# One of four bank assignments, one read and the transposes in a two-layer block-product kernel

## The chip, the cores and the metric

The kernel runs on one NeuronCore of a Trainium2 chip. The metric is the device time of one execution in microseconds. The kernel before took 1352.98 us, the median of three runs (1351.76, 1352.98 and 1362.14). The profile is of a further execution, which took 1365.32 us.

Engines are called as in the profile: PE is TensorE (the matrix engine), PEld its loading of weights, DVE is VectorE, ACT is ScalarE, POOL is GpSimd, and SP is SyncE, which here only issues DMAs. An engine works through its own queue in order. It stops at an instruction until the semaphores that this one waits for have been reached, and all that stands behind it waits too.

## The reference

The input x has 32 batches of 64 channels and 1024 positions. A table of 16 matrices of 64 x 64 is indexed by a condition per batch. A feed-forward layer follows, and its result is added to x.

```python
W = weights[condition]                          # (32, 64, 64)
y = einsum('bct,bcd->bdt', x, W)                # (32, 64, 1024)
h = gelu(einsum('bsd,df->bsf', y, inter_w) + inter_b, approximate=True)   # F = 4096
x + einsum('bsf,fd->bsd', h, output_w) + output_b
```

All is in float32. Seen as matrices, layer one multiplies 2048 x 1024 by 1024 x 4096, layer two 2048 x 4096 by 4096 x 1024.

## The kernel before

**Blocks.** Both layers use a scheme of seven block products in place of eight (sums of blocks are formed first, and each product is added to several results), and use it twice, one inside the other. So 49 small products replace 64. The outer seven stand in `OUTER` (line 25: 1, 2, 6, 7, 4, 5, 3) in the order in which they are computed, the inner seven in `INNER` (lines 30 to 38). A line of `INNER` gives a slot (its time inside the block), the product's number, the PSUM tag, whether it starts a new accumulation, and the sub-block of the result. The state tables (`STATE`, `MID_STATE` and those for the end) say which results a product is added to: X, V, D in layer one, X, Y, Z, D in layer two.

**Passes.** Layer one makes eight passes (`it`): two halves of the rows times four groups of columns. Layer two makes seven outer products (`o` from 0 to 6), and each product there sums over the four groups of columns. A pass is 49 units of time, and a unit is one product. In the trace a product is eight PE rows of 128 x 256, because each float32 matmul shows as two; names beginning with f (`fA`, `fB`, `fC`) are products of layer one, with z of layer two, and the letter after it is the PSUM tag. Names with X, V, D, Y or Z after f or m (`fX`, `mZ`) are results in SBUF.

**PSUM.** [...] The pool `pst` holds two under the tag t, for copies of left and right sums. The pool `acc_pool` holds two for each of the tags A, B and C. `INNER` puts one product per block on B (slot 1, read in slot 2), one accumulation on C (slots 2 and 5, read in slots 3 and 6), and the rest on A. A tag's two banks are given out in turn, and a bank is free when the readers of its former tile are through. VectorE takes one operand of a sum from PSUM, so ScalarE first copies the other operand there (`to_psum`, lines 199 to 207, ACT at L206).

**Order.** The order is written out by hand. `at(time, fn, ...)` (line 177) collects steps, `run` (line 180) sorts them by time and calls them. What a step issues goes to the end of its engines' queues. Times set only the order. A tile is allocated when its step is called.

**Layer one, end of a block.** `hidden` (lines 588 to 644) is called for outer products 2, 4, 5 and 3, whose results are complete. For each of the sub-blocks "11" = (0,0), "21" = (0,1), "22" = (1,1) and "12" = (1,0) it applies the gelu (`do_gelu`, ACT at L569). In the passes of the second half of the rows (`it >= NG`, passes 4 to 7) it then forms an inner sum in place: `inner_s1_copy` copies the lower half of the tile into a C bank, and `inner_s1` adds it to the upper half on VectorE. After these come the outer sums (a1 to a6) and the stores of the results to DRAM (`hs_d`).

**Layer two.** `product3` issues a product, `read3` moves or adds its result: the first time it is a ScalarE copy (L941), otherwise a VectorE sum. `inner_h2` forms inner sums of the left operand (`hs`) from ScalarE copies and VectorE sums. When a block of an outer result is complete, `outer_copy` and `outer3` add the outer results. For outer products 2, 4, 5 and 3 the result then goes out: `transpose` (line 1024) makes four PE transposes into a tile `tp` on a B bank, `add_x` adds it to a tile `xb` of x that `load_xb` has fetched, and `store_out` stores it. The pool of `xb` has four tiles, so a load waits until the store of the tile four before it has landed. In the last blocks the tile of x is called `xe`.

**Queues.** All of layer two's loads are issued by SP: the left operands (`load_h`, L811), the weights (`load_w`, L817), `xb` (L1021), and so are the stores (L1042). GpSimd forms sums of whole left operands and weights (`mid_h`, `mid_w`, `inner_w2`) in the order of the tables `POOL2` and `POOL2_END`, lines 1053 to 1063.

Of the kernel before, what the change touches and what calls it, by code (L numbers as in the profile page):

```python
# [24 lines left out]
OUTER = (1, 2, 6, 7, 4, 5, 3)  # L25
# [50 lines left out]
def kernel(  # L76
# [37 lines left out]
    B, C, T = x.shape  # L114
# [62 lines left out]
    def at(time, fn, *args):  # L177
        steps.append((time, len(steps), fn, args))
# [6 lines left out]
    def add(eng, o, a, b, sub=False):  # L185
        eng.tensor_tensor(o, a, b, ALU.subtract if sub else ALU.add)  # L186
# [12 lines left out]
    def to_psum(src, tag=None):  # L199
        uid[0] += 1  # L200
        pool = late["acc"] if tag else pst
        t = pool.tile([P, 2, W], F32, tag=tag or "t", name=f"t{uid[0]}")
        if len(src.shape) == 2:
            t = t.rearrange("p k n -> p (k n)")
        t = t[:, : src.shape[1]]
        nc.scalar.copy(t, src)  # L206
        return t
# [280 lines left out]
    def y_block(a, p, r):  # L488
        q = Y[a, RIGHT[p]]
        return {"11": blk(q, 0, 0), "21": blk(q, 1, 0)}.get(r) if r in ("11", "21") else YI[a, p][r]  # L490

    def w1_block(it, p, l):
        q = W1[it, LEFT[p]]
        return {"11": lblk(q, 0, 0), "12": lblk(q, 0, 1)}.get(l) if l in ("11", "12") else WI[it, p][l]
# [66 lines left out]
    H = {}  # L561

    def gelu(it, fin, sub):
        s = it % NG
        t = state[fin[0], sub]
        H[it, fin, sub] = t
        for u in range(2):
            f = 8 * s + 4 * fin[1][0] + 2 * sub[0] + u
            nc.scalar.activation(  # L569
                t[:, u, :], t[:, u, :], AF.Gelu_apprx_tanh, bias=b1[:, f : f + 1]  # L570
            )

    S1 = {}

    def inner_s1_copy(it, fin, sub):
        S1[it, fin, sub] = to_psum(H[it, fin, sub][:, 1, :], "C")

    def inner_s1(it, fin, sub):

# [8 lines left out]
    def hidden(base, it, fin):  # L588


        v = nc.vector
        subs = {"11": (0, 0), "12": (1, 0), "21": (0, 1), "22": (1, 1)}
        e = {}

        def get(n):
            H[it, fin, n] = e[n] = H[it, fin, subs[n]]

        def new(n):
            H[it, fin, n] = e[n] = cpool.tile(
                [P, 2, W], F32, tag="c", name=f"h{n}_{it}_{fin[1][0]}{fin[1][1]}"  # L600
            )

        def do_gelu(n):
            gelu(it, fin, subs[n])
            get(n)

        def a1():
            e["p"] = to_psum(e["21"])

        def a2():  # L610
            new("s3")
            add(v, e["s3"], e["11"], e["p"], sub=True)

        def a3():
            add(v, e["21"], e["p"], e["22"])
            H[it, fin, "s1"] = e["s1"] = e["21"]
            e["p"] = to_psum(e["11"])

        def a4():
            new("s2")  # L620
            add(v, e["s2"], e["s1"], e["p"], sub=True)

        def a5():
            e["p"] = to_psum(e["12"])
            new("s4")

        def a6():
            add(v, e["s4"], e["p"], e["s2"], sub=True)

        for n, t in (("11", 2.9), ("21", 6.9), ("22", 7.9), ("12", 12.9)):  # L630
            at(base + t, do_gelu, n)
            if it >= NG:
                at(base + t + 0.01, inner_s1_copy, it, fin, subs[n])
                at(base + t + 0.45, inner_s1, it, fin, subs[n])
        at(base + 8.3, a1)
        at(base + 9.3, a2)
        at(base + 9.6, a3)
        at(base + 10.6, a4)
        at(base + 13.4, a5)
        at(base + 14.4, a6)  # L640
        for n, t in (
            ("11", 4.2), ("22", 9.2), ("s3", 10.5), ("s1", 11), ("s2", 12), ("12", 14.2), ("s4", 15.6),
        ):
            at(base + t, store_h, it, fin, n)
# [52 lines left out]
    for j, i in enumerate(order):  # L697
        t = M_AT[i]
# [18 lines left out]
    for j, t in enumerate(later):  # L717
        i = NR - NL + j
# [14 lines left out]
    for it in range(nit):  # L733
# [5 lines left out]
        for n, t in W_AT.items():  # L739
            if it == 0:  # L740
                t = {1: -10, 2: -3.5, "s3": -3, "s1": -2}.get(n, t)
# [4 lines left out]
        for o, p in enumerate(OUTER):  # L746
# [3 lines left out]
                lambda l, r, it=it, p=p, a=a: (w1_block(it, p, l), y_block(a, p, r)),  # L750
            )
            fin = STATE[p][1]
# [6 lines left out]
        if it == 1:  # L759
            for k in range(KQ):  # L760
                e = {}
                t = b0 + 5 + 10.8 * k
# [3 lines left out]
        elif it >= 2:  # L766
            n = -(-len(w2_pieces) // (nit - 2))
            for j in range(n):
                i = (it - 2) * n + j
                if i < len(w2_pieces):  # L770
                    e = {}
                    t = b0 + 9.5 + 14 * j
# [61 lines left out]
    def mid_s3(time, o, t):  # L834

        e = {}

        def one(k):
            if k == 0:
                pool, tag = (wpool, "w") if (o, t) == (6, 1) else (yq, "yq")  # L840
                HT[o, "s3", t] = pool.tile([P, NG, 2, W], F32, tag=tag, name=f"hs3_{o}_{t}")
            e[k] = to_psum(HT[o, "s2", t][:, k])

        def two(k):
            add(nc.vector, HT[o, "s3", t][:, k], HT[o, "22", t][:, k], e[k], sub=True)

        for k in range(NG):
            at(time + 0.8 * k, one, k)
            at(time + 0.8 * k + 0.6, two, k)
# [59 lines left out]
    def mids(o):  # L909
        return MID_END if o == 6 else MID  # L910
# [36 lines left out]
    def add_copy(time, dst, src):  # L947

        e = {}

        def one():
            e["p"] = to_psum(src(), "C")

        def two():
            add(nc.vector, dst(), e["p"], dst())

        at(time, one)
        at(time + 0.6, two)
# [105 lines left out]
    for o in range(7):  # L1064
        b = end1 + 49 * o
        pick = lambda later, first=None: b + (first if o == 0 else later)
        for (n, t), tt in H_LOAD.items():
            at(pick(*tt), load_h, o, n, t)
        for n, tt in W_LOAD2.items():
            at(pick(*tt), load_w, o, n)  # L1070
        for n, k, *tt in POOL2_END if o == 6 else POOL2:
            if n == "w":
                at(pick(*tt), inner_w2, o, mids(o)[k])
            elif n[0] == "t":
                at(pick(*tt), mid_w, o, n)
            else:
                at(pick(*tt), mid_h, o, n, k)
        mid_s3(b + (18.9 if o == 6 else 24), o, 0)
        mid_s3(b + (22.2 if o == 6 else 28), o, 1)
        for i, q in enumerate(mids(o)):  # L1080
            bq = b + 7 * i
            inner_h2(bq - 2.2 if (o, i) != (0, 0) else bq + 0.7, o, q)
            rs = INNER
            if (o, i) in ((6, 5), (6, 6)):

                at(bq + 7.01, read3, o, i, (6, 7, "A", False, (1, 0)))
                rs = INNER[:-1] + ((7, 4, "B", True, (1, 0)),)
            for r in rs:
                at(bq + r[0], product3, o, i, r)
                at(bq + r[0] + 1, read3, o, i, r)  # L1090
            if q == MID_SUM:
                parts = ((0, slice(0, 2), 7.1), (1, slice(0, 2), 12.1))
                if o == 6:
                    parts = (parts[0], (1, slice(1, 2), 7.2), (1, slice(0, 1), 12.1))
                for t, c, f in parts:
                    add_copy(
                        bq + f,
                        lambda o=o, t=t, c=c: MS[o, "Z", t][:, c, :],
                        lambda o=o, t=t, c=c: MS[o, "X", t][:, c, :],
                    )  # L1100
            for j, (src, mb) in enumerate((MID_DONE_END if o == 6 else MID_DONE).get(q, ())):
                for t in range(2):
                    if (o, i) == (6, 6):

                        add_copy(
                            bq + (1.2, 2.3)[t],
                            lambda o=o, t=t: MS[o, "Z", t],
                            lambda mb=mb, t=t: OS["X", mb, t],
                        )
                        at(bq + 4, ends_in, o, mb, t)  # L1110
                    f = bq + (7.1, 8.1 if (o, i) == (6, 5) else 12.2)[t] + j
                    if (o, i) != (6, 6):
                        at(f, outer_copy, o, src, mb, t)
                        at(f + 0.7, outer3, o, src, mb, t)
                    if STATE[OUTER[o]][1] is None:
                        continue
                    at(b + 33 if (o, mb, t) in ENDS else f - 1.8, load_xb, o, mb, t)
                    if (o, i) == (6, 6):
                        continue
                    at(f + 2.2, transpose, o, mb, t)  # L1120
                    at(f + 3.2, add_x, o, mb, t)
                    at(f + 4, store_out, o, mb, t)
# [52 lines left out]
```

## Time and profile before

| what | us |
|---|---|
| median of three runs | 1352.98 |
| profiled execution | 1365.32 |
| its span, first to last instruction | 1363.5 |
| PE busy | 1340.6 |
| VectorE busy | 882.7 |
| GpSimd busy | 959.7 |
| ScalarE busy | 487.2 |
| mean granted PE clock over the span | 0.991 |

Busy time is the union of an engine's instructions in the profiled execution. A PE row's duration contains its way through the array and overlaps the next row, so the distance from start to start is the better measure of a stream of matmuls. The list of waits gives, for an engine and a line, what ended its idle time, how long that was in total, how often, and the longest. The timeline merges neighbouring instructions of one kind; the number in brackets is the engine's idle time before them and what ended it. The view of stretches gives, for each engine, its busy time and number of instructions, and then the granted PE clock, the mean busy share of the 16 DMA engines, and GB/s.

### The profile page before, as it was taken

The numbers are of one execution on the slowest core, as the hardware profiler recorded it, in microseconds if no ns is written. First come the engines' busy times: TensorE is split into PE (matmuls) and PEld (weight loads), VectorE is DVE, ScalarE is ACT, GpSimd is POOL, SyncE is SP. The second block draws the span as 40 slices with busy tenths as digits, with TensorE's granted clock in tenths as the row PEclk, the third lists the DMA queues.
The fourth block names the chain that finished last, engine by engine and source line by source line (L and its number), as shares of the span: only waits on it lengthen the run. The fifth ranks groups of instructions, "written<-read, shape, count | busy, mean of one in ns | idle before, by whom it ended". The sixth has DMA issues, their size and how long they took to land.

```text
span 1363.5 us, 19040 instructions
## 1 busy us (share of the span) xinstructions
PE 1340.6 (98%) x6572; PEld 1174.7 (86%) x6572; DVE 882.7 (65%) x1581; ACT 487.2 (36%) x985; POOL 959.7 (70%) x599
## 2 busy tenths in 40 slices
PE   8899999999999999999999999999999999999998
PEld 8788888888888888888888888888888888888887
DVE  1757457575687765756647674775766757767676
ACT  1533324233254341533515332433334333333341
POOL 3772954948659587495762976958959689496692
PEclk7999999999999999999999999999999999999999
DMA  5655578586898767667659236173270723917611
GB/s 194 197 172 190 172 219 286 208 288 220 284 362 273 237 218 248 241 222 244 229 191 332 70 123 264 45 296 139 96 275 7 290 97 112 359 32 257 222 47 62
DMA packets 135472, 273.40 MB, mean 201 GB/s; under 512 B 15728, under 2 KB 68208, under 8 KB 123728
## 3 DMA queue, kind: packets, MB, share of 16 engines
q1 hardware_dynamic: 134336, 271.53, 57.4%
q8 instruction: 53, 0.87, 0.2%
q0 software_dynamic: 448, 0.46, 0.1%
q14 instruction: 43, 0.35, 0.1%
q10 hardware_dynamic: 592, 0.20, 0.1%
HBM read 167.28 MB, written 104.86 MB: 200 GB/s over the span
## 4 chain that ended last, share of the span: by engine, by line
PE 53%; DVE 2%; POOL 1%; DMA 1%; issue 1%; ACT 1%; SPq 0%; DVEq 0%; ACTq 0%; POOLq 0%
PE zA L555 24%; PE zC L555 12%; PE zB L555 6%; PE fA L544 6%; PE fC L544 3%; PE fB L544 1%; PE tp L1031 1%; DVE hs L186 1%; DMA w2p<-in_L_ffn_output_w_dram 0%; POOL w2p L186 0%; POOL ws L186 0%; DVE mZ L186 0%; DVE mX L186 0%; ACT o L974 0%; DMA hs_d<-hs 0%
## 5 line engine op out<-in xcount | busy, mean ns | idle before, releaser
L544 PE MATMUL fA<-yi,wi 128*128 128x256 f32 x896 | 213.9, 382 | 2.5 <-DVE fD L186 1.1
L186 DVE TENSOR_TENSOR hs<-h,t 128x512 f32<-128x512 f32 x308 | 200.2, 680 | 6.1 <-ACT t L206 3.1
L555 PE MATMUL zA<-hs,wt 128*128 128x256 f32 x840 | 197.8, 379 | 0.0
L186 POOL TENSOR_TENSOR h<-h,h 128x1024 f32<-128x1024 f32 x84 | 196.1, 2362 | 0.4 <-DMA h<-hs_d 0.4
L544 PEld LDWEIGHTS fA<-yi,wi 128*128 128x128 f32 x896 | 170.3, 191 | 28.4 <-DVE fX L186 1.9
L555 PEld LDWEIGHTS zA<-hs,wt 128*128 128x128 f32 x840 | 158.4, 190 | 20.9
L186 POOL TENSOR_TENSOR wi<-w 128x512 f32<-128x512 f32 x80 | 101.8, 1272 | 50.1 <-PE fC L544 24.5
L569 ACT ACTIVATE fD<-fD,b 128x256 f32<-128x256 f32 x128 | 57.9, 500 | 185.5 <-DVE fD L186 181.0
L186 POOL TENSOR_TENSOR ws<-w,w 128x1024 f32<-128x1024 f32 x32 | 74.9, 2362 | 68.6 <-PE fA L544 58.3
L206 ACT COPY t<-h 128x512 f32<-128x512 f32 x140 | 81.8, 590 | 75.3 <-DVE hs L186 71.2
L206 ACT COPY t<-hs 128x512 f32<-128x512 f32 x112 | 65.4, 588 | 108.1 <-DVE hs L186 108.1
L186 POOL TENSOR_TENSOR wt<-v 128x512 f32<-128x512 f32 x35 | 44.6, 1274 | 83.3 <-DMA v<-w_d 80.1
L186 DVE TENSOR_TENSOR fX<-fA,fX 128x512 f32<-128x512 f32 x104 | 71.4, 686 | 44.5 <-PE fA L544 44.4
L186 POOL TENSOR_TENSOR wi<-w,wi 128x512 f32<-128x512 f32 x40 | 50.9, 1271 | 62.6 <-PE fA L544 55.8
L544 PE MATMUL fC<-y,wi 128*128 128x256 f32 x352 | 83.3, 380 | 0.1
L555 PE MATMUL zC<-hs,v 128*128 128x256 f32 x336 | 79.5, 379 | 1.3 <-ACT mX L941 1.3
L555 PE MATMUL zA<-h,wt 128*128 128x256 f32 x320 | 75.6, 379 | 0.0
L544 PE MATMUL fA<-yi,w 128*128 128x256 f32 x320 | 75.6, 379 | 0.0
L544 PEld LDWEIGHTS fC<-y,wi 128*128 128x128 f32 x352 | 66.7, 190 | 9.5 <-issue 0.5
L555 PEld LDWEIGHTS zC<-hs,v 128*128 128x128 f32 x336 | 63.7, 190 | 10.2 <-ACT mX L941 1.7
L186 POOL TENSOR_TENSOR wt<-v,wt 128x512 f32<-128x512 f32 x35 | 44.5, 1271 | 34.9 <-PE zA L555 34.9
L555 PEld LDWEIGHTS zA<-h,wt 128*128 128x128 f32 x320 | 60.8, 190 | 8.3
(185 smaller groups left out, 2830.9 us busy)
## 6 DMA issues: line engine op xcount, KB each, us to landing
h<-hs_d SPq DMA_DIRECT2D x56, 1024.0 KB
w<-in_L_ffn_inter_w_dram SPq DMA_DIRECT2D x32, 1024.0 KB
hs_d<-hs SPq DMA_DIRECT2D x96, 256.0 KB
v<-w_d SPq DMA_DIRECT2D x21, 1024.0 KB
hs_d<-fD SPq DMA_DIRECT2D x64, 256.0 KB
w2p<-in_L_ffn_output_w_dram SPq DMA_DIRECT2D x32, 512.0 KB
w_d<-w2p SPq DMA_DIRECT2D x64, 256.0 KB
w_d<-w2t SPq DMA_DIRECT2D x48, 256.0 KB
```

The costliest lines, as they stand in the source:

```text
L186: eng.tensor_tensor(o, a, b, ALU.subtract if sub else ALU.add)
L206: nc.scalar.copy(t, src)
L544: nc.tensor.matmul(acc[:, u, :], lt[:, k, ts(u, P)], rt[:, k, :], start=start and u == 0 and k == 0, stop=k == 1, skip_group_check=True,)
L555: nc.tensor.matmul(acc, wl[:, k, :], hr[:, k, :], start=start and k == 0, stop=k == NG - 1, skip_group_check=True,)
L569: nc.scalar.activation(t[:, u, :], t[:, u, :], AF.Gelu_apprx_tanh, bias=b1[:, f : f + 1])
L1031: nc.tensor.transpose(tp[:, v, ts(n0, P)], d[:, n0, ts(v, P)], late["ident"])
```

## The change

There are three parts.

1. In `inner_s1_copy` the copy for the sub-block (0,1) takes a B bank; the other three stay on C. The steps of the sub-block "12" are moved from 12.91 to 13.02 (the copy) and from 13.35 to 13.32 (the sum).
2. The first read of a C product in layer two, (`o`, `i`, slot) = (0, 0, 2), is put at 0.3 units behind its product instead of 1.
3. The steps `transpose`, `add_x` and `store_out` of a complete result come 0.3 units later, and 1.2 units later in the block of outer product 5. `load_xb` stays where it is.

```diff
     def inner_s1_copy(it, fin, sub):
-        S1[it, fin, sub] = to_psum(H[it, fin, sub][:, 1, :], "C")
+        tag = "B" if sub == (0, 1) else "C"
+        S1[it, fin, sub] = to_psum(H[it, fin, sub][:, 1, :], tag)
...
             at(base + t, do_gelu, n)
             if it >= NG:
-                at(base + t + 0.01, inner_s1_copy, it, fin, subs[n])
-                at(base + t + 0.45, inner_s1, it, fin, subs[n])
+                t += 0.12 if n == "12" else 0.01
+                at(base + t, inner_s1_copy, it, fin, subs[n])
+                at(base + t + (0.3 if n == "12" else 0.44), inner_s1, it, fin, subs[n])
...
             for r in rs:
                 at(bq + r[0], product3, o, i, r)
-                at(bq + r[0] + 1, read3, o, i, r)
+                at(bq + r[0] + (0.3 if (o, i, r[0]) == (0, 0, 2) else 1), read3, o, i, r)
...
                     at(b + 33 if (o, mb, t) in ENDS else f - 1.8, load_xb, o, mb, t)
                     if (o, i) == (6, 6):
                         continue
+                    f += 1.2 if OUTER[o] == 5 else 0.3
                     at(f + 2.2, transpose, o, mb, t)
                     at(f + 3.2, add_x, o, mb, t)
                     at(f + 4, store_out, o, mb, t)
```

On PE, VectorE and SP the order of instructions changes by this in the following places only. In the block of `o` = 5 (outer product 5) each group of four transposes and its `add_x` move behind the next product or the next read. On SP, in the blocks of outer products 2, 4 and 5, stores of results move behind loads of `xb`, and in the block of 5 one also behind a load of weights (`vt`) and one behind a load of a left operand (`h`). On ScalarE one copy of layer two moves ahead of two others. On GpSimd nothing moves.

## The prediction, made before the changed kernel was run

> **What bounds the kernel now.** I read the page's first part, then TensorE's waits, then the timeline around each wait. The page says where the time is:
>
> ```profile
> span 1363.5 us, 19040 instructions
> PE 1340.6 (98%) x6572; PEld 1174.7 (86%) x6572; DVE 882.7 (65%) x1581; ACT 487.2 (36%) x985; POOL 959.7 (70%) x599
> ```
>
> TensorE (PE) is busy for 98% of the span. The change removes no matmul, so it can only act on the 23 us in which PE stands, and on time in which PE is slow. PE's waits name the places (total us, times, longest):
>
> ```profile
> PE py L322 <- issue: 6.1, 4, 5.2
> PE tp L1031 <- DVE xb L186: 3.1, 3, 2.2
> PE fC L544 <- DVE fV L186: 2.5, 3, 0.8
> PE zC L555 <- ACT mX L941: 1.3, 1, 1.3
> ```
>
> The first line is the start-up mix, which the diff does not touch. The other three are its three parts, 6.9 us together. For each I ask what is late next. One product is eight PE rows, 1.73 us from start to start (744.93 and 746.66); that is one unit of the order's times.
>
> **Part 1, the copy that moves to B's banks.** The stall stands at 476.95, 562.74 and 649.89, once in the last block of each of three passes, always alike (start, duration, engine, line; in brackets the idle time):
>
> ```profile
> 474.06 0.41 DVE L186 TENSOR_TENSOR fD<-t,fD 128x256 f32<-128x256 f32 x1
> 474.23 1.89 PE L544 MATMUL fB<-y,w 128*128 128x256 f32 x8
> 476.37 0.42 DVE L186 TENSOR_TENSOR fV<-t,fV 128x256 f32<-128x256 f32 x1 [0.71 <-ACT t L206]
> 476.95 1.96 PE L544 MATMUL fC<-y,w 128*128 128x256 f32 x8 [0.82 <-DVE fV L186]
> 477.31 0.68 DVE L186 TENSOR_TENSOR fX<-fA,fX 128x512 f32<-128x512 f32 x1
> 478.75 1.89 PE L544 MATMUL fA<-yi,wi 128*128 128x256 f32 x8
> ```
>
> fC needs a C bank, and that one holds the copy of sub-block (0,1), read by the fV sum that ends at 476.79. In the changed program this copy stands in a B bank; fC's bank was last read by the fD sum, which ends at 474.47. So fC starts when fB is through, at 474.23 + 1.73 = 475.96, and ends at 477.69. Next is fA<-yi,wi: it overwrites the half of the A bank that VectorE's fX<-fA reads until 477.99. That sum stands behind fV and hs on VectorE, and both still wait for the same ScalarE copies, whose order doesn't change. With the hand-over of 0.16 us (476.79 to 476.95), fA starts at 478.15 instead of 478.75. The first matmul after a stop costs about 0.07 more (fC took 1.80 to the next, not 1.73), and this stop stays, one product later. So 0.53 us a time, 1.6 us for three. Bounds: 0 if the sum of fX slips as far as fC comes forward, 3.0 if it comes forward too. I take 1.6, from the rows.
>
> Copies are neither added nor removed (0.38 us each, and their sums 0.42). The fourth copy goes from 12.91 to 13.02 and passes nothing on ScalarE or VectorE. B's banks carry one product per block, read two slots after its start, so the copy finds one free and the next fB finds the other; PE gets no wait from it. I cost that at nothing. If fB had to wait for the copy's sum, it would be some tenths in each of 16 blocks.
>
> **Part 2, the read put ahead.** The first product pair of layer two:
>
> ```profile
> 752.32 0.59 ACT L206 COPY t<-hs 128x512 f32<-128x512 f32 x1
> 752.84 0.37 ACT L941 COPY mX<-zC 128x256 f32<-128x256 f32 x1
> 752.94 0.69 DVE L186 TENSOR_TENSOR hs<-h,t 128x512 f32<-128x512 f32 x1 [0.66 <-ACT t L206]
> 753.26 1.99 PE L555 MATMUL zC<-hs,v 128*128 128x256 f32 x8 [1.26 <-ACT mX L941]
> ```
>
> mX<-zC would then run right after the zC product, at about 750.4, past two copies that wait for VectorE, and zC<-hs could start at 751.84. But hs is its operand. The second half of it is the hs sum at 752.94, which needs the copy at 752.32, and that copy waits for a VectorE sum that starts at 751.61; nothing there gets earlier. The four left rows of the product need that half: 753.63 + 0.16 = 753.79, then 4 x 0.216 and a restart of 0.07 give 754.7, against 755.09 where the next product starts now. Gain 0.4, bounds 0 and 1.4. The wait moves into the middle of the product.
>
> **Part 3, the transposes.** The long wait is in the block of outer product 5:
>
> ```profile
> 1264.17 0.37 SPq L1021 DMA_DIRECT2D xb<-in_x_dram  x1
> 1264.42 0.60 PE L1031 MATMUL tp<-ident,mX 128*128 128x128 f32 x4
> 1264.85 1.89 PE L555 MATMUL zB<-h,v 128*128 128x256 f32 x8
> 1267.63 0.68 DVE L186 TENSOR_TENSOR hs<-h,t 128x512 f32<-128x512 f32 x1
> 1268.22 0.69 DVE L186 TENSOR_TENSOR xb<-tp,xb 128x512 f32<-128x512 f32 x1
> 1268.83 0.41 DVE L186 TENSOR_TENSOR mX<-zB,mX 128x256 f32<-128x256 f32 x1
> 1268.97 0.66 PE L1031 MATMUL tp<-ident,mY 128*128 128x128 f32 x4 [2.22 <-DVE xb L186]
> 1269.46 3.56 PE L555 MATMUL zC<-h,v 128*128 128x256 f32 x8
> ```
>
> The transpose of mY needs the B bank of the one at 1264.42, whose reader is at the end of a full VectorE queue. And zC then takes 3.35 us to the next start instead of 1.73. The stretches show why (PE busy, further on the granted clock, DMA share, GB/s):
>
> ```profile
> 1269.00:1273.00 4.00, 4.00 (x14) 3.18 (x15) 0.93 (x2) 0.00 (x0) 0.00 (x0) 0.57 0.98 355
> ```
>
> The clock fell to half. The place costs 2.39 (zB through at 1266.58, transpose at 1268.97) + 1.62 (zC) + 0.13 (slow transposes) = 4.1 us.
>
> [...]
>
> After the change tp(mX) stands behind zB, and one product lies between it and the next transpose. PE: zB 1264.42 to 1266.15, tp to 1266.58, zC to 1268.31. The transpose of mY now needs the bank of zB, whose reader is mX<-zB; it takes the slot after hs on VectorE, 1268.22 to 1268.64. The two adds that also moved fill gaps that VectorE has before 1261 (0.93 and 1.04 us), so the queue is not longer. PE stands from 1268.31 to 1268.8: 0.5, with the restart 0.6. Shown gaps up to 1.26 us kept the clock at 1.00. Gain 4.1 - 0.6 = 3.5; bounds 1.8 (no slow clock in an ordinary run) and 4.1.
>
> The steps bring their DMAs. On SP the store of (1,1) moves behind the loads of xb (1,0) and of vt; the load of xb (0,1) waits for that store to land (it reuses its buffer), and behind this load stand the 1 MB loads of h22 and v22. SP waits 5.3 us there already (for a store issued at 1256.37, landed 1264.15 by the landing records). The DMA is full at 400 GB/s, so with 1.25 MB put ahead the store lands at about 1267.5, and h22 is issued at 1268 instead of 1264.6. The queue is then nearly empty, so 4.6 us (1228.99 to 1233.98 and the like) give a landing at about 1273 instead of 1271.7. GpSimd adds it at 1276.51 today, waiting for PE until 1275.28; it will start at 1273.3. What PE needs of this chain, the sum for zC at 1296.20, is ready at 1290.5 now: 5.7 us of cover. PE comes 3.5 us earlier and GpSimd 3.2, so 5.3 are left. In the blocks of 2 and 4 only SP's order changes, by one 256 KB transfer (0.65 us), under the same cover; PE's stalls of 0.42 at 920.18 and 1178.16 stay.
>
> **Sum.** 1.6 + 0.4 + 3.5 = 5.5 us. The profiled execution took 1365.3 us (span 1363.5 and 1.8 around it), so 1359.8 by its own time. It is 12.3 us above the median of 1353.0; the other runs spread from 1351.8 to 1362.1, and the 5.2 us wait at 65 us, untouched, may be part of that. The stalls follow from orders on the engines, so I carry the difference over: 1353.0 - 5.5 = 1347.5 us.
>
> **Rivals.** (a) The waits move on fully: the fX sum, the hs half and the next transpose take the stalls over, and only the slow clock (1.6) and half the long gap (1.2) go. For it: all three parts show a successor. 1353.0 - 2.8 = 1350.2. (b) The three waits go entirely, as the wait list suggests: 3.0 + 1.4 + 4.1 = 8.5, 1344.5. Against it: the successor rows above. (c) Slower: SP stands behind the late store and h22 lands late. From 1278.6 (the start that GpSimd's chain needs) PE waits one for one; the 5.5 us are eaten at 1284, 11 us after my estimate; 3.4 us more, and 1.6 for a halved clock, would give 1358. Against it: the DMA, which is free by then. (d) Order without effect: outside outer product 5 the later times change no PE order; if an ordinary run has no half clock, 1349.2.
>
> **How the numbers follow.** My forecast, with (d) as its upper part, 0.66; (a) 0.17; (b) 0.10; (c) 0.07. The runs of one kernel differ by 10 us and a median of three may fall on the slow side, so the range goes from 1343.5, just under (b), to 1355.5. A measurement of this kernel tells about 1% (13.5 us) from no change; no case reaches it by its own mechanism, only together with that spread: faster 0.07, same 0.87, slower 0.06.
>
> **What would show it.** Right: no fC wait on fV; three waits of fA on fX of about 0.3 to 0.5 us; a wait of about 1 us inside zC<-hs at 753; no half clock near 1270, and a wait of about 0.5 of tp on mX. Wrong: GpSimd waiting for h22 beyond 1278, a wait of fB on a copy's sum, or the half clock again.

## The result, and the profile after

The changed kernel takes 1352.51 us, the median of 22 runs (1345.87 to 1360.64); the kernel before, run 22 times by then, 1362.14 us (1351.76 to 1364.19). The ratio of the times is 0.9956 with a 95% interval from 0.9938 to 0.9975: faster by 5.9 us of 1353, between 3.4 and 8.4. The medians lie 9.6 us apart, because the runs of both kernels fall into two groups, 8 to 9 us apart, and the kernel before had 14 of 22 in the upper one, the changed kernel 10. Inside the groups the medians differ by 3.9 us (1354.0 and 1350.2) and by 4.9 us (1363.2 and 1358.3). What makes the groups is settled by an experiment below. The profiled execution took 1358.5 us and belongs to the upper group, as that of before does.

The page of the changed kernel begins:

```profile
span 1356.7 us, 19035 instructions
PE 1337.3 (99%) x6572; PEld 1173.7 (87%) x6572; DVE 882.9 (65%) x1581; ACT 487.8 (36%) x985; POOL 959.7 (71%) x599
```

Of TensorE's waits (total us, times, longest), those of fC on fV and of zC on mX are gone, and four rows stand where the change acts:

```profile
PE fA L544 <- DVE fX L186: 1.5, 4, 0.6
PE zA L555 <- DVE mX L186: 1.0, 1, 1.0
PE tp L1033 <- DVE xb L186: 0.9, 2, 0.4
PE zC L555 <- DVE hs L186: 0.8, 1, 0.8
```

**Part 1.** The timeline at the first of the three places, 475 us (start, duration, engine, line, operation; in brackets the idle time):

```profile
473.73 1.89 PE L544 MATMUL fC<-y,w 128*128 128x256 f32 x8
475.08 0.68 DVE L186 TENSOR_TENSOR fX<-fA,fX 128x512 f32<-128x512 f32 x1
475.91 1.97 PE L544 MATMUL fA<-yi,wi 128*128 128x256 f32 x8 [0.29 <-DVE fX L186]
```

fC runs through, and the next product on A waits 0.29 us for the sum of fX. With the slow first matmul (1.97 us for the eight rows, 1.89 for those of fC) the stop costs 0.53 us where it cost 1.06. The other two places show 0.29 us too. Gain 1.6 us.

**Part 2.** The wait has moved into the product:

```profile
748.00 1.03 PE L555 MATMUL zC<-hs,v 128*128 128x256 f32 x4
749.11 0.69 DVE L186 TENSOR_TENSOR hs<-h,t 128x512 f32<-128x512 f32 x1 [0.66 <-ACT t L206]
749.85 1.13 PE L555 MATMUL zC<-hs,v 128*128 128x256 f32 x4 [0.82 <-DVE hs L186]
```

Four matmuls run, and the second four wait 0.82 us for the sum that ends at 749.80. The place costs 1.08 us after 1.53: gain 0.45.

**Part 3.** TensorE in the block of outer product 5:

```profile
1260.14 1.89 PE L555 MATMUL zB<-h,v 128*128 128x256 f32 x8
1261.87 0.60 PE L1033 MATMUL tp<-ident,mX 128*128 128x128 f32 x4
1262.30 1.89 PE L555 MATMUL zC<-h,v 128*128 128x256 f32 x8
1264.30 0.66 PE L1033 MATMUL tp<-ident,mY 128*128 128x128 f32 x4
```

The transpose of mY starts 2.00 us after zC, so after 1.73 us of product it stood 0.27 us, for mX<-zB on VectorE. The clock stays full (1.00 over 1264.30:1268.30). The place costs 0.33 us with the slow first matmul, where it cost 4.14 us before: gain 3.8.

**A new wait.** The zA row of the waits above was not forecast. Where it arises:

```profile
1295.89 1.28 DVE L186 TENSOR_TENSOR hs<-h,t 128x512 f32<-128x512 f32 x2 [1.52 <-POOL h L186]
...
1300.30 3.22 DVE L186 TENSOR_TENSOR hs<-h,t 128x512 f32<-128x512 f32 x5
...
1303.43 0.42 DVE L186 TENSOR_TENSOR mX<-zA,mX 128x256 f32<-128x256 f32 x1
...
1303.99 1.32 PE L555 MATMUL zA<-hs,wt 128*128 128x256 f32 x5 [1.02 <-DVE mX L186]
```

VectorE stood 1.52 us for a sum of GpSimd. Its sums of hs came late, and mX<-zA, which empties an A bank, stands behind five of them in VectorE's queue. TensorE waits for that bank: 1.02 us, with the restart about 1.25.

The rest of the difference of the two spans (6.8 us) is not the change's: 1.6 + 0.45 + 3.8 - 1.25 = 4.6, and the profiled execution of after is 2.2 us ahead at 126 us, before any instruction that the change moves.

### The profile page after: what moved, and what is told of

It reads as the page before. It is cut to its first block, busy times and chain, and to the rows that moved or that the text cites. A ratio compares the mean times of both kernels' runs of the same rounds, so it can differ in the third digit from the quotient of the medians.

```text
span 1356.7 us, 19035 instructions
## 1 busy us (share of the span) xinstructions
PE 1337.3 (99%) x6572; PEld 1173.7 (87%) x6572; DVE 882.9 (65%) x1581; ACT 487.8 (36%) x985; POOL 959.7 (71%) x599
## 4 chain that ended last, share of the span: by engine, by line
PE 50%; DVE 3%; POOL 2%; issue 1%; DMA 1%; ACT 1%; SPq 0%; DVEq 0%; POOLq 0%; ACTq 0%
PE zA L555 22%; PE zC L555 11%; PE fA L544 6%; PE zB L555 6%; PE fC L544 3%; PE fB L544 1%; DVE hs L186 1%; POOL h L186 1%; PE tp L1033 1%; DMA w2p<-in_L_ffn_output_w_dram 0%; DMA out_dram<-xb 0%; POOL w2p L186 0%; POOL vt L186 0%; ACT t L206 0%; POOL ws L186 0%
## 5 line engine op out<-in xcount | busy, mean ns | idle before, releaser
L544 PEld LDWEIGHTS fA<-yi,w 128*128 128x128 f32 x320 | 60.9, 190 | 8.2
```

What stands on the lines that cost most here:

```text
L544: nc.tensor.matmul(acc[:, u, :], lt[:, k, ts(u, P)], rt[:, k, :], start=start and u == 0 and k == 0, stop=k == 1, skip_group_check=True,)
```

## The experiments

**Parts 1 and 2 without part 3.** The edit is the first two parts of the diff:

```diff
-        S1[it, fin, sub] = to_psum(H[it, fin, sub][:, 1, :], "C")
+        tag = "B" if sub == (0, 1) else "C"
+        S1[it, fin, sub] = to_psum(H[it, fin, sub][:, 1, :], tag)
...
-                at(bq + r[0] + 1, read3, o, i, r)
+                at(bq + r[0] + (0.3 if (o, i, r[0]) == (0, 0, 2) else 1), read3, o, i, r)
```

> Parts 1 and 2 on the kernel before, without part 3. Site theory (each part acts only at its own waits): the three waits of fC on fV are gone and three waits of fA on fX of about 0.29 us stand in their place (gain 1.6 us), the wait at 753 moves into the product (gain 0.45), the wait of the transpose of mY near 1269 stays at 2.2 us with the half clock behind it, and there is no wait of zA on mX near 1304 to 1308. Sum 2.0 us, span about 1361.5 if the start-up is as in the profile of before. Rival for the clock: the half clock behind the 2.2 us wait was chance, then zC behind it runs at 1.73 us here and the place costs 2.4 instead of 4.1 us.

One execution took 1351.36 us, with a span of 1349.6. The sites behave as expected: three waits of fA on fX of 0.29, 0.82 inside zC<-hs, 2.22 for the transpose of mY, none of zA on mX. The clock does not. First this kernel behind the 2.2 us wait, on TensorE and in the stretch of 4 us (PE busy, further on the granted clock):

```profile
1256.71 0.66 PE L1033 MATMUL tp<-ident,mY 128*128 128x128 f32 x4 [2.22 <-DVE xb L186]
1257.20 1.89 PE L555 MATMUL zC<-h,v 128*128 128x256 f32 x8
1256.70:1260.70 4.00, 3.99 (x23) 3.58 (x24) 1.67 (x3) 0.37 (x1) 0.00 (x0) 1.00 0.97 362
```

The same wait, and the clock stays at 1.00: zC takes its 1.73 us. A run described further down, of the order of before, shows the other case:

```profile
1260.43 0.66 PE L1031 MATMUL tp<-ident,mY 128*128 128x128 f32 x4 [2.22 <-DVE xb L186]
1260.92 3.21 PE L555 MATMUL zC<-h,v 128*128 128x256 f32 x8
1260.50:1264.50 4.00, 4.00 (x15) 3.26 (x16) 0.90 (x2) 0.33 (x1) 0.00 (x0) 0.60 0.98 333
```

Six profiles have this wait of 2.22 us. The table shows what the granted clock did behind it; where a stretch stands beside it, its mean granted clock is given. (e3, e5, e9 and e10 are described below.)

| profile | wait, us | clock behind it |
|---|---|---|
| before | 1266.75 to 1268.97 | half for 3.41 us (0.50 over 1269.52:1272.93) |
| e3, order of before here | 1265.54 to 1267.76 | half for 3.41 us |
| e5, order of before here | 1258.92 to 1261.14 | half for 3.41 us |
| e9, order of before here | 1258.21 to 1260.43 | half for 3.41 us (0.60 over 1260.50:1264.50) |
| e1, parts 1 and 2 | 1254.49 to 1256.71 | full (1.00 over 1256.70:1260.70) |
| e10, parts 1 and 2 | 1256.36 to 1258.58 | full (1.00 over 1258.60:1262.00) |

So a wait of the same length had the half clock behind it in four profiles and the full clock in two: its length does not tell which. In e6 a wait of 2.00 us, up to the py at 67.74, had slow rows behind it too: four matmuls of fB at 69.67 took 1.63 us, where the first four of zC at 748.00 in the changed kernel took 1.03. What tells the cases apart was not shown.

The cases do not look like chance. All four profiles with the order of before lose the clock, and neither of the two with parts 1 and 2 does. These two parts bring the wait about 2.0 us forward: it begins 894.50 us behind the 2000th row of TensorE in e9, 892.46 in e10. By these six profiles parts 1 and 2 by themselves also end the half clock, 1.7 us on top of their 2.05, and part 3 is worth only 2.1 us where they are already in. No run moved this wait and nothing else, so this is read from the profiles and not isolated.

**Part 3 alone.**

```diff
+                    f += 1.2 if OUTER[o] == 5 else 0.3
                     at(f + 2.2, transpose, o, mb, t)
```

> Part 3 alone on the kernel before. Site theory: the wait of 2.2 us and the half clock near 1269 are gone (gain 3.85), the new wait of zA on mX of 1.0 us stands about 4 us behind its place in the changed kernel (cost 1.25), the three waits of fC on fV stay at 0.82. Net gain 2.6 us, ratio to before 0.998. Rival (the clock keeps full speed in ordinary runs): gain 2.2 - 1.25 = 1 us, ratio 0.9993.

The ratio to before is 0.9986 with an interval from 0.9965 to 1.0006, 1.9 us, which does not tell 2.6 from 1. The trace tells more: no wait and no half clock near 1269, three waits of fC of 0.82, and the new wait of zA on mX is 2.05 us, twice as long as in the changed kernel. From the trace that is 3.8 - 2.3 = 1.5 us of gain, in keeping with the 1.9. The new wait varies with the execution.

**Part 3 with 0.3 units everywhere**, so that near 1269 only SP's order changes:

```diff
+                    f += 0.3
                     at(f + 2.2, transpose, o, mb, t)
```

> Part 3 with 0.3 units in every block, so that in the block of outer product 5 only SP's order changes and no transpose passes a product. PE-order theory: the wait of 2.2 us near 1269 stays and the span is that of before within 0.5 us; no wait of zA on mX near 1308, since PE, held by the 2.2 us, leaves GpSimd its cover. SP-order rival: the late stores by themselves make GpSimd late, and the wait near 1308 of about 1 us appears here too.

One execution took 1364.11 us, its span is 1362.3 against 1363.5. That is 1.2 us where 0.5 was allowed, and 1.17 us of it stand before 100 us, ahead of every changed step. The 2.22 us wait and the half clock are there, a wait of zA on mX is not. So this much of SP's order gains nothing and costs nothing. It is not all of it: the first store (1255.16) still goes out ahead of the loads of xb and vt, which it stands behind in the changed kernel. That order without TensorE's was not tried.

**The second load of h22 early**, in the changed kernel:

```diff
-            at(pick(*tt), load_h, o, n, t)
+            at(b + 4.05 if (o, n, t) == (6, "22", 1) else pick(*tt), load_h, o, n, t)
...
+                    tx = b + 33 if (o, mb, t) in ENDS else f - 1.8
+                    if OUTER[o] == 5 and (mb, t) == ((0, 1), 1):
+                        tx += 0.8
+                    at(tx, load_xb, o, mb, t)
```

> The changed kernel with the second load of h22 of the last block put on SP ahead of the last load of xb and of the three stores before it (SP's order only). Theory (the new wait of zA on mX at 1304 comes from h22's second load standing behind the load that waits for a store): the load is issued at about 1269 instead of 1273.29 and lands at about 1275, GpSimd does not wait 0.97 us for it, and the wait of 1.02 us at 1304 goes or falls under 0.3; the span is 1.0 to 1.25 us shorter, ratio to before about 0.9947 against 0.9956 for the changed kernel. Rival (the first half of h22, or VectorE's queue alone, sets the wait): the wait at 1304 stays within 0.2 of 1.02 us and the time is that of the changed kernel.

First SP and GpSimd in the changed kernel:

```profile
1271.80 0.37 SPq L1023 DMA_DIRECT2D xb<-in_x_dram  x1
1272.26 0.93 SPq L1044 DMA_DIRECT2D out_dram<-xb  x2
1273.29 0.48 SPq L813 DMA_DIRECT2D h<-hs_d  x1
...
1280.43 4.67 POOL L186 TENSOR_TENSOR h<-h,h 128x1024 f32<-128x1024 f32 x2 [0.97 <-DMA h<-hs_d]
```

SP stood until 1271.80 for a store of xb to land (the store of block (1,0), part t = 0, issued at 1264.77 where it was issued at 1258.43 before). The load of h behind it was issued at 1273.29 and landed at 1280.37, and GpSimd waited for it. The same in this run, whose times lie 7.56 us earlier in this part:

```profile
1261.33 0.33 SPq L813 DMA_DIRECT2D h<-hs_d  x1
1262.20 0.61 SPq L1023 DMA_DIRECT2D xb<-in_x_dram  x1
...
1270.96 4.66 POOL L186 TENSOR_TENSOR h<-h,h 128x1024 f32<-128x1024 f32 x2
```

The load goes out first, lands at 1268.67, GpSimd does not wait, and TensorE has no wait of more than 0.2 us from 1200 to 1340. The one profile could be luck, since one of the four with the changed order and the load in its old place (e11 below) has no wait either. But e7 and e12, which also have the load early, have none, and the three that have the wait are all of the old place. With GpSimd's wait for the load gone in the trace, the load's place is shown as a cause. The time says less: median 1351.51 us, ratio to before 0.9942 (0.9924 to 0.9961), against 0.9956 for the changed kernel.

How much room the chain has can be read from six profiles. The distance is from the start of the h sum above to the time at which zA was due on TensorE (7.35 us behind the start of the zA<-hs,wt before it, as where nothing waits):

| profile | sum starts | zA due | distance | zA late by |
|---|---|---|---|---|
| before | 1285.78 | 1310.89 | 25.11 | 0 |
| e4, h22 early | 1270.96 | 1295.26 | 24.30 | 0 |
| e11, see below | 1270.86 | 1294.81 | 23.95 | 0 |
| changed kernel | 1280.43 | 1302.82 | 22.39 | 1.17 |
| e6, see below | 1278.95 | 1300.81 | 21.86 | 1.74 |
| e2, part 3 alone | 1285.94 | 1307.30 | 21.36 | 2.22 |

In the last three rows distance and lateness add up to 23.56, 23.60 and 23.58. So the chain needs about 23.6 us, and before it had 25.11: 1.5 us of cover.

**The first gather early**, on the kernel before and on the changed kernel. Six rows of x are mixed inside layer one, each with weights that GpSimd gathers:

```diff
-        at(7.5 + 3 * j, gather, i)
+        at(7.5 + 3 * j if j else -3.25, gather, i)
```

> The kernel before with the gather for the first of the six later rows (the weights of the start-up mix) moved on GpSimd ahead of the 14 us of weight sums that it stands behind. Theory (the two groups of times, 1352 to 1357 and 1361 to 1366 for the kernel before, are runs without and with PE's wait of about 5 us for this gather near 60 us and the half clock behind it): only the lower group is left, all runs under 1359, median about 1355, ratio about 0.996. Rival (the groups come from the start-up loads themselves): the wait near 60 us goes, but two groups stay and the ratio is over 0.998.

> The changed kernel with the same early gather. With the groups gone, the change is to be read from this run and the one of before with the early gather: theory, 1350 against 1355, so 4 to 5.5 us (1.6 + 0.45 + 2.4 to 3.9 for the transposes, by whether the clock halves behind the 2.2 us wait, less 0 to 2 us for the new wait of zA on mX near 1300). Rival (part of the 0.44% was the mix of the groups): under 3 us.

Of the kernel before, all 22 runs with the early gather lie between 1355.89 and 1360.06, while the 38 runs of the kernel before in the same comparison have 18 between 1362.98 and 1365.96. The upper group is gone, so the wait for this gather is what made it. The marks set for the time were missed: five runs lie over 1359, and the median is 1357.70 where about 1355 was expected; the lower group of the kernel before has its median at 1356.9 in this comparison. In the profile of the changed kernel gather and product stand like this:

```profile
57.42 0.96 POOL L262 DMA_INDIRECT wsel_l<-in_L_cond_weights_dram,rows  x1 [0.16 <-issue]
...
63.13 3.68 PE L322 MATMUL py<-wsel_l,xl 64*128 64x64 f32 x32 [4.66 <-issue]
```

TensorE stood from 58.5 on and got the weights 5.7 us after the gather was issued; the clock was at half for 6.8 us from 62.18. An estimate from these figures is 4.7 us of standing and half of the 5.9 us from 63.13 on, 7.6 us in all, near the distance of the groups. In e1 and e4, both in the lower group, the gather went out at 54.0 and 54.4 and there was no wait for it. There GpSimd's sums ahead of it had begun at 34.7 and 35.1, when a load of weights landed, not at 38.1 to 40.3. Why that load lands later in some executions was not tried. Ratios to before: 0.9977 (0.9963 to 0.9991) and 0.9952 (0.9933 to 0.9972), medians 1357.70 and 1354.96. The difference of the medians, 2.7 us (3.7 of the means), lies under the expected 4 to 5.5 and inside the rival's under 3. The profile of the second has a wait of 2.00 us for the next gather, which the profile of the first has not, and a new wait of zA on mX of 1.58; so this pair does not settle the size, and the next one moves both gathers.

**Two additions to the changed kernel.** With the early gather and h22's load early, first an early read of the first A product in the last block of passes 4 to 6, and then also 1.2 units for the transposes in the blocks of 2 and 4:

```diff
-            at(base + (slot + 1) * unit, read, blkno, key, q, nm)
+            early = slot == 0 and blkno % 7 == 6 and NG <= blkno // 7 < 2 * NG - 1
+            at(base + (slot + (0.3 if early else 1)) * unit, read, blkno, key, q, nm)
```

```diff
-                    f += 1.2 if OUTER[o] == 5 else 0.3
+                    f += 1.2
```

> The changed kernel with the early gather, with h22's second load early, and with the read of the first A product of the last block of passes 4 to 6 put 0.3 units behind it, ahead of two sums on VectorE that wait for ScalarE. Theory: the three waits of fA on fX of 0.29 us go (1.6 us), the wait near 1300 goes (0 to 1.25 us), so 1.6 to 2.9 us under the changed kernel with the early gather, about 1347.5 to 1348.5. Rival: the sums put behind the early read pass their lateness on to the next product on C or A, and no more than 0.5 us comes.

> The same with the 1.2 units for the transposes in the blocks of outer products 2 and 4 too. Theory: PE's two waits of 0.43 us of tp on xb there shrink to about 0.1 (0.7 us in sum), if GpSimd has cover there; 0.7 us under the run before. Rival (what the later stores did in the block of 5): the load of xb that waits for a store holds back h22 in these blocks as well, and up to two new waits of about 1 us of zA on mX appear, so 0 to 2 us over the run before.

The first gives 1351.21 us (7 runs; ratio 0.9925, 0.9899 to 0.9952), 3.7 us under e6, where 1.6 to 2.9 was expected. Its trace has neither the three waits of fA on fX near 480, 560 and 650 nor one of zA on mX. The second gives 1354.10 (9 runs; 0.9944, 0.9920 to 0.9968). Its two waits of tp on xb are gone (0.85 us), but TensorE's waits have a row that none of the others shows:

```profile
PE zA L556 <- POOL wt L186: 1.5, 1, 1.5
```

It stands at 954, with two waits of zB on GpSimd's v of 0.33 us at 963 and 1223. The later transposes make GpSimd's operands late in those blocks too, as the rival had it. The load of h that SP issued at 923.95, behind a load of xb that waited until 921.67, held GpSimd for 1.97 us before 932.42; in e7 GpSimd has no such wait there. The place where TensorE stands is another than the rival said. This profile also has 2.9 us for the second gather, so not all of the 2.9 us between the medians is from the transposes.

**Both gathers early.**

```diff
-        at(7.5 + 3 * j, gather, i)
+        at(7.5 + 3 * j if j > 1 else -3.25 + 0.05 * j, gather, i)
```

> The kernel before with the gathers for the first two later rows moved ahead of the weight sums on GpSimd (the run with one gather moved left a wait of up to 2.9 us of PE for the second in two of four profiles). Theory: no wait of py for a gather after 30 us, one group of times, spread under 4 us. This is the base for the next three. Rival: the second wait was not the gather, and stays near 67 us.

> Parts 1 and 2 alone on the kernel before; here with the same two gathers moved. [...]

> The changed kernel with the two gathers moved. Theory: 2.0 us (parts 1 and 2) + 2.4 to 3.9 (the transposes) - 0.5 to 2.3 (the new wait of zA on mX of 0 to 2 us) = 2.4 to 5.4 us under the base with the gathers, middle 4. Prediction's sum: 5.5. Rival (the measured 0.44% is the mix of groups): under 2 us.

> The changed kernel with the two gathers, h22's second load early and the early read in passes 4 to 6. Theory: 1.6 us for the three waits plus 0.5 to 2.3 for the wait near 1300, so 2 to 4 us under the run before, 6 to 8 under the base with the gathers. Rival: the parts overlap and under 1 us comes.

The kernel that ran as e10 has its gathers in the old place, other than its text says: it is parts 1 and 2 alone on the kernel before, in 22 runs, and is compared with that. The kernel before had 47 runs here, median 1360.34.

| | median us | runs | ratio to before | interval |
|---|---|---|---|---|
| e9, before with both gathers | 1355.23 | 22 | 0.9962 | 0.9948 to 0.9976 |
| e10, parts 1 and 2, gathers as before | 1353.65 | 22 | 0.9975 | 0.9957 to 0.9992 |
| e11, changed kernel with both gathers | 1350.45 | 10 | 0.9935 | 0.9913 to 0.9958 |
| e12, all additions but the last | 1347.76 | 6 | 0.9902 | 0.9870 to 0.9933 |

All 22 runs of e9 lie within 5.5 us (1351.72 to 1357.21), a little more than the 4 expected, and no wait for a gather of a later row is left in its profile. From e9 to e11 is the change without the groups: 4.8 us by the medians, 4.5 by the means (22 and 10 runs), inside the expected 2.4 to 5.4. e10 gains 3.4 us of before (1.1 to 5.8), which holds both the 2.05 that the two parts gain at their own waits (1.6 + 0.45) and the 3.75 that the end of the half clock would make of it; its own runs still have the two groups. e12 is 2.7 us under e11 and beats both kernels: 12.6 us under the median of before, 1.0% by the ratio.

## Why the prediction was right and wrong

**What failed is the step from the sum to the forecast.** The sum of 5.5 us is 0.41% of the time. The text then said that a measurement of this kernel tells about 1% from no change, and put 0.87 on no change. With 22 runs of each kernel the 95% interval is 0.19% to either side, 2.5 us. So 5.5 us is over twice what can be told, and by its own sum the forecast had to be faster. The 1% was taken from the 10 us between three runs, but that spread is mostly two groups with one removable cause.

**The base was mis-sized.** 1353.0 came from three runs, two of them in the lower group. Of 22 runs 14 are in the upper one, and the median is 1362.14. The text saw that the start-up wait near 65 us might be part of the spread, and it was most of it: with both gathers moved, 5.5 us of spread are left (e9). That the measured 1352.51 lies in the range is owed partly to a base that was too low and a mix of groups that favoured the changed kernel.

**Part 1** is right: 1.6 us, the same successor, nothing from the move to the B banks (no wait of fB on a copy's sum). **Part 2** is right: 0.4 said, 0.45 measured, inside the product.

**Part 3** gained 3.8 in the profiles compared, where 3.5 was said. The text counted the row in full (4.1), slow clock included, and put its lower bound of 1.8 and rival (d) on an ordinary run that has no half clock. No profile with the order of before shows that: all four bear the row out, and there its way of counting was right. What it missed is that the three parts do not add up: parts 1 and 2 bring the wait 2.0 us forward, and in both profiles that have them alone the clock stays full and the place costs 2.4 us. So the 1.7 us of the slow clock belong to either, once. The sum for all three parts does not change by that.

**The cover of GpSimd failed as a term.** The text allowed GpSimd 5.7 us, by the product zC at 1296.20, and left 5.3 after the change. The consumer that comes due first is another one: GpSimd's h sum, the hs sums on VectorE, mX<-zA behind them in the same queue, and TensorE's A bank. That way the cover is 1.5 us. The text followed only the first half of h22; it was issued at 1264.25 and landed at 1269.97, no later than before, though GpSimd then stood 2.09 us for it, since TensorE had freed GpSimd sooner. The second half, behind the load that waits for the late store, it did not follow. Its own sign of being wrong, GpSimd waiting for h22, came true there: 0.97 us, until 1280.43. The cost is 0 to 2.2 us: 1.17, 2.22, 1.74 and 0 in the four profiles with this order, 1.3 in the mean. It is a small form of rival (c), with the mechanism that (c) named (SP behind the late store) and another way to TensorE.

Put together: 1.6 + 0.45 + 3.8 - 1.3 = 4.6 us, where 5.5 was said and 4.8 was measured without the groups (and 5.9, 3.4 to 8.4, with them). Rivals (a) and (b) fall by the traces: each wait left the successor that the text gave it, neither the whole of it nor nothing. Rival (d) needed an ordinary run of the kernel before to keep its clock; none of the four profiles with its order does.

## What to carry to other kernels

Compare a small sum with the interval that many runs give, not with the spread of a few, and look in the profile for what splits the runs: here one gather behind 14 us of sums on another engine. When a step is moved later, follow each load behind its DMA to the engine that consumes it, and from there through that engine's queue to all that stands behind: the tightest consumer was three queues away. When a fix removes a wait of TensorE, expect that the other engines have lost that much time to be ready in, and give them their loads earlier in the same edit. And when two fixes act on one chain, ask whether the first moves the place of the second, as parts 1 and 2 did here with the clock.

## What the runs showed of the hardware

- A wait of TensorE of 2.22 us had half clock behind it for 3.41 us in four profiles (before: 0.50 over 1269.52:1272.93) and the full clock in two (e1: 1.00 over 1256.70:1260.70; e10: 1.00 over 1258.60:1262.00). Behind one of 2.00 us in e6 four matmuls took 1.63 us where four take 1.03 at full clock. What tells these cases apart was not shown.
- A gather of 128 rows on GpSimd's queue was issued in 0.96 us, and its data reached TensorE 5.5 to 5.9 us after the issue began in the four profiles in which TensorE waited for the first one (57.42 to 63.13 in the changed kernel).
